# Six blocks of weight quantization in front of a delta-rule scan, and its PSUM banks dealt out anew

## The chip, the core and the metric

The kernel runs on one core of a Trainium2 chip. The metric is the device time of one execution in microseconds (us). The core has five engines with a queue each, worked in order: TensorE for matmuls (PE, with PEld for its weight loads), VectorE (DVE), ScalarE (ACT), GpSimd (POOL) and SyncE (SP), which here only issues transfers. Matmuls write to PSUM, which has eight banks; a bank holds 128 x 512 float32 values.

## The reference

Two transformer-like layers with modulation (`adaLN`) over 2 sequences of 1024 tokens of width 512. Only the first layer's first half bears on this change.

```python
mod = (silu(c0) @ wmod0).reshape(2, 6, 1, 512)      # sa, ca, ga, sb, cb, gb of layer 0
h = layernorm(x) * (1 + ca) + sa
x = x + ga * L0_attn(h)          # delta rule: k, q, v, alpha from h; a 64 x 64 state per sequence
h = layernorm(x) * (1 + cb) + sb
x = x + gb * L0_ffn(h)           # weights made ternary in groups of 64 rows
...
def ternary_quant(w, g=64):      # in bf16
    scale = clip(mean(abs(w_g)), 1e-8)
    q = clip(round(w_g / scale), -1, 1)
    return q * scale
```

The delta rule is a scan over tokens: each step reads the state with q and k, forms an error, a "surprise" gate from it, and updates the state. `L0_ffn` is silu(gate) * up, an RMS norm, and a projection; its `w_gate_up` (4096 x 512) and `w_proj` pass through `ternary_quant`. The second layer (an RWKV-like scan and a feed-forward part with integer weights) follows with modulation vectors of its own.

## The kernel before

**The scan of layer 0.** The 1024 tokens of each sequence are cut into NC = 16 chunks of TT = 64; both sequences lie side by side on the 128 partitions. GT = 2 chunks form a group, so there are NG = 8 groups. A group passes four functions:

- `project(g)` (L309): layer norm on DVE, POOL and ACT, transposes on PE (`pt_a`), the modulated `hTa` on ACT (L338), the projections `pk` (L346) and `pv` (L360), and the normalised `kqr` on DVE (L385, L386).
- `pairs(g, ...)` (L389): the interactions of a chunk's tokens among each other, by doubling over six levels. It starts with `kl` (L396) and `pd`; each level is a PE product `pg`, a predicated copy (L419) and three products on DVE (L428, L431, L437). At its end come `pe`, `pm2`, `pse`, `pki` and `pik`, each followed by one ACT or DVE instruction. All of these PE results have the one tag `pg` in pool `ps_g` with one buffer, so that one bank holds them, one after another.
- `delta_chunk` (L536), twice: about ten short steps between PE, ACT and DVE (`wa` L544, the squares L486, `rt` L494, `r` L496, the new state `h` L518, `w` L553), and checks `miss` and `size` for a fallback branch, which is not run with these inputs.
- `attention_out` (L590): `pssy`, a power on POOL (L236), two products `poa`, and for each a residual on DVE (`res_a`, L229) and an addition to x on POOL (L230). `poa` has one PSUM buffer.

Beside these, two kinds of filling work belong to a group: `modulation(n)` (L680), which makes the next n of ten modulation vectors (sixteen matmuls at L149, a copy at L154, then L161 or L171 and their readers), and `quantize(n)` (L697), which takes the next n of 32 blocks of `w_gate_up` through `ternary` (L649). A block is a load of 256 KB on SP's queue (`qst`, two buffers), Abs and Sign on ACT (`q_ab` L659, `q_sg` L661), one matmul that sums over 64 rows (`pm`, L663), a scaled copy on ACT (`q_sc`, L665), five DVE instructions (`q_d` and `q_m`, L669 to L674) and a cast on ACT (L675). The PSUM results of modulation and quantization share pool `ps_q`, with two buffers.

The order of the main loop, and how far ahead things are written, is this:

```python
ops = [pairs(0, *project(0))]
modulation(1)
ahead = [project(1)]
for g in range(NG):
    ...                       # two delta_chunks of group g
    ...                       # pairs up to g + 2, project up to g + 3, attention_out(g)
    modulation((1, 1, 1, 1, 1, 2, 1, 1)[g])
    quantize(ND)              # ND = 4 blocks
```

**What sets the order on an engine.** The order of the statements is not yet that of the queues. When the kernel is built, a planner deals the instructions to each engine's queue by its own estimate of when they are ready, and among those that are ready the one written earlier goes first. So filling work slips between steps of a chain, and a part of the text written further up gets precedence. On the chip each queue then runs strictly as dealt.

**PSUM in the scan.** Pools: `ps_p` 2 banks (projections), `ps_g` 1 (pairs), `ps_q` 2, `ps_u` 2 (chunks), `ps_o` 1 (outputs). When the scan is over, the pool stack `sp` is closed and the banks go to the feed-forward part, whose first transposes and whose tile `hh` (L219) wait until the scan's tiles are let go.

**Loads of x.** `load_x(c0, c1)` issues one transfer for each sequence. Chunks 0 and 1 are loaded first, then, after the first weights, chunks 2 and 3, and right behind them chunks 4 to 15 at once.

Of the kernel before, what the change touches and what calls it, by code (L numbers as in the profile page):

```python
# [8 lines left out]
F32 = mybir.dt.float32  # L9
# [5 lines left out]
PSUM = bass.MemoryType.PSUM  # L15

P = 128
B, S, D = 2, 1024, 512
ND = D // P
TT = 64  # L20

NC = S // TT
GT = 2
# [19 lines left out]
def block_pair_kernel(ctx: ExitStack, tc: tile.TileContext, a: dict, out: bass.AP):  # L43
    nc = tc.nc

    def pool(stack, name, bufs=1, **kw):
        return stack.enter_context(tc.tile_pool(name=name, bufs=bufs, **kw))
# [66 lines left out]
    def run(general, rs):  # L114
# [136 lines left out]
        with ExitStack() as la:  # L251
# [5 lines left out]
            sp = ExitStack()  # L257
# [1 line left out]

            ps_p = pool(sp, "ps_p", bufs=2, space=PSUM)  # L260
            ps_g = pool(sp, "ps_g", bufs=1, space=PSUM)
            ps_q = pool(sp, "ps_q", bufs=2, space=PSUM)
            ps_u = pool(sp, "ps_u", bufs=2, space=PSUM)
            ps_o = pool(sp, "ps_o", bufs=1, space=PSUM)
            proj = work = pool(sp, "proj", bufs=1)
# [123 lines left out]
            def pairs(g, kqr, al, v):  # L389

                gm = gms[g % 3]
                kqv = kqr.rearrange("p i (j t) -> p i j t", j=GT)
                gmv = gm.rearrange("p (j i) t -> p j i t", j=GT)
                kl = pair.tile([P, GT, TT], F32, tag="kl", name=f"kl_{g}", bufs=2)
                klf = kl.rearrange("p j t -> p (j t)")
                nc.vector.scalar_tensor_tensor(  # L396
                    klf, al, 1.0, kqr[:, 0], ALU.subtract, ALU.mult
                )

                pd = ps_g.tile([P, GT, TT], F32, tag="pg", name=f"pd_{g}")  # L400
                for j in range(GT):
                    both(pd[:, j], kl[:, j], kqv[:, 1, j])
                nc.vector.copy_predicated(
                    gmv[:, :, 2, :], mdiag.unsqueeze(1).to_broadcast([P, GT, TT]), pd
                )

                tot = al
                for h in LEVELS:  # L410
                    nb = TT // (2 * h)
                    ps = ps_g.tile([P, GT, 3, TT // 2], F32, tag="pg", name=f"pg_{g}_{h}")
                    right = kqr.rearrange("p i (n two h) -> p i n two h", two=2, h=h)[:, :, :, 1, :]
                    for j in range(GT):
                        both(
                            ps[:, j].rearrange("p i (n h) -> p i n h", h=h), kl[:, j],
                            right[:, :, j * nb:(j + 1) * nb, :],
                        )
                    nc.vector.copy_predicated(  # L419
                        gm.rearrange("p i (n two h) -> p i n two h", two=2, h=h)[:, :, :, 1, :],  # L420
                        masks[h].rearrange("p (n h) -> p n h", h=h).unsqueeze(1).to_broadcast(
                            [P, GT * 3, nb, h]
                        ),
                        ps.rearrange("p j i (n h) -> p (j i) n h", h=h),
                    )
                    tv = tot.rearrange("p (n two) -> p n two", two=2)
                    left = klf.rearrange("p (n two h) -> p n two h", two=2, h=h)[:, :, 0, :]
                    nc.vector.tensor_tensor(  # L428
                        left, left, tv[:, :, 1].unsqueeze(2).to_broadcast([P, GT * nb, h]), ALU.mult
                    )  # L430
                    nc.vector.tensor_tensor(  # L431
                        right, right,
                        tv[:, :, 0].unsqueeze(1).unsqueeze(3).to_broadcast([P, 3, GT * nb, h]),
                        ALU.mult,
                    )
                    nxt = pair.tile([P, GT * nb], F32, tag=f"tot{h}", name=f"tot_{g}_{h}")
                    nc.vector.tensor_tensor(nxt, tv[:, :, 0], tv[:, :, 1], ALU.mult)  # L437
                    tot = nxt
                atot = scan.tile([P, GT], F32, tag="atot", name=f"atot_{g}", bufs=3)
                nc.vector.tensor_copy(atot, tot)  # L440
                pe = ps_g.tile([P, GT, 3, TT], F32, tag="pg", name=f"pe_{g}")
                for j in range(GT):
                    both(pe[:, j, 0], kl[:, j], eye)
                    both(pe[:, j, 1], gmv[:, j, 0], eye)
                    both(pe[:, j, 2], kqv[:, 0, j], eye)

                kem = scan.tile([P, GT, 3, TT], F32, tag="kem", name=f"kem_{g}", bufs=3)
                nc.scalar.copy(kem, pe)

                im = pair.tile([P, GT, TT], F32, tag="im", name=f"im_{g}")  # L450
                nc.gpsimd.tensor_tensor(
                    im, gmv[:, :, 0], eye.unsqueeze(1).to_broadcast([P, GT, TT]), ALU.add
                )
                pm2 = ps_g.tile([P, GT, TT], F32, tag="pg", name=f"pm2_{g}")
                for j in range(GT):
                    both(pm2[:, j], gmv[:, j, 0], kem[:, j, 1])
                m2 = pair.tile([P, GT, TT], F32, tag="m2", name=f"m2_{g}")
                nc.scalar.copy(m2, pm2)
                pse = ps_g.tile([P, GT, TT], F32, tag="pg", name=f"pse_{g}")
                for j in range(GT):  # L460
                    both(pse[:, j], m2[:, j], im[:, j])
                inv = scan.tile([P, GT, TT], F32, tag="inv", name=f"inv_{g}", bufs=3)
                nc.vector.tensor_tensor(inv, pse, im, ALU.add)

                pki = ps_g.tile([P, GT, 2, TT], F32, tag="pg", name=f"pki_{g}")
                for j in range(GT):
                    both(pki[:, j, 0], kem[:, j, 2], inv[:, j])
                    both(pki[:, j, 1], inv[:, j], eye)
                ki = scan.tile([P, GT, 2, TT], F32, tag="ki", name=f"ki_{g}", bufs=3)
                nc.scalar.copy(ki, pki)  # L470
                pik = ps_g.tile([P, GT, TT], F32, tag="pg", name=f"pik_{g}")
                for j in range(GT):
                    both(pik[:, j], ki[:, j, 1], kem[:, j, 0])
                ik = scan.tile([P, GT, TT], F32, tag="ik", name=f"ik_{g}", bufs=3)
                nc.scalar.mul(ik, pik, 0.5)
                return gmv, kqv, kem, inv, atot, v, ki, ik
# [123 lines left out]
            def scan_all(chunk, p, name):  # L600
                h = p.tile([P, DS], F32, tag="h", name=f"h_init{name}")
                nc.vector.memset(h, 0.0)
                state[0] = h
                ops = [pairs(0, *project(0))]
                modulation(1)
                ahead = [project(1)]
                for g in range(NG):
                    yT = scan.tile([P, GT, TT], F32, tag="yT", name=f"yT_{g}{name}")
                    ysq = scan.tile([P, GT, TT], F32, tag="ysq", name=f"ysq_{g}{name}")
                    for j in range(GT):  # L610
                        chunk(GT * g + j, j, ops[g], yT, ysq)

                    for n in range(len(ops), min(g + 3, NG)):
                        ops.append(pairs(n, *ahead[n - 1]))
                        if n == g + 1:
                            attention_out(g, yT, ysq, f"{g}{name}")
                        for n in range(len(ahead) + 1, min(n + 2, NG)):
                            ahead.append(project(n))
                    if g:
                        attention_out(g, yT, ysq, f"{g}{name}")  # L620
                    modulation((1, 1, 1, 1, 1, 2, 1, 1)[g])
                    quantize(ND)
# [21 lines left out]

            nc.vector.tensor_scalar(wo, wo, nw, -1.0, ALU.mult, ALU.mult)
            load_x(GT, 2 * GT)
            load_x(2 * GT, NC)

            def ternary(dst, src, psp, tag, name):  # L649

# [29 lines left out]
            def modulation(n):  # L680

                for layer, key in later[:n]:
                    if key == "sa1":
                        mods["sc1"] = cond(1)
                    i = ("sa", "ca", "ga", "sb", "cb", "gb").index(key[:2])
                    sc = mods["sc1"] if layer else sc0
                    rows = mod_rows(load_wmod(layer, i, nc.sync), ps_q, "q", sc, key, w0a)
                    if key[0] == "g":
                        to = w0a if key == "ga0" else const if layer else w0
                        mods[key] = mod_gate(rows, ps_q, "q", key, to)  # L690
                    else:
                        mods[key] = mod_cols(rows, ps_q, "q", key, key[0] == "c")
                del later[:n]
# [340 lines left out]
        with ExitStack() as lr:  # L1034
# [105 lines left out]
            ahead = tokens(1)  # L1140
# [208 lines left out]
```

## Time and profile before

| | |
|---|---|
| median of 3 runs | 1224.29 us (1224.22 to 1228.45) |
| the profiled execution | 1233.09 us, of which its span 1231.2 us |
| PE busy | 1138.4 us, 92% of the span |
| PEld busy | 854.5 us, 69% |
| DVE busy | 730.3 us, 59% |
| ACT busy | 636.8 us, 52% |
| POOL busy | 410.4 us, 33% |
| first matmul of `gu` (L762) | at 299.65 us |

All durations below come from the one profiled execution, which took 0.7% longer than the median. Busy shares are means over stages that differ much, so each stage has to be read by itself. A busy PE is one that has matmuls in its pipeline, not one at its peak. The granted clock of PE (PEclk) is given as a share of full speed. In the chain of waits each piece is what released the next one, followed back from the last instruction.

### The profile page before, as it was taken

Reading aid. Unit: us, or ns where it says so; the run is one execution under the profiler, and the core shown is the slowest. Engines: PE = TensorE matmul, PEld = TensorE weight load, DVE = VectorE, ACT = ScalarE, POOL = GpSimd, SP = SyncE. Lnnn points to the kernel's source line nnn. Section 1 sums busy time; section 2 is a strip of 40 time slices with the busy share of each in tenths; the row PEclk is TensorE's granted clock in tenths of the full one; section 3 lists DMA queues with packets and bytes.
Section 4 is the critical chain, followed back from the end, with each engine's and each line's share of the span. In section 5 each row is a group of like instructions: output and inputs, shape, how many; then the busy total and the mean of one; then the engine's idle time right before and its main releaser. Section 6 shows DMA issues by size and latency. Waiting matters only on the chain.

```text
span 1231.2 us, 17856 instructions
## 1 busy us (share of the span) xinstructions
PE 1138.4 (92%) x6746; PEld 854.5 (69%) x6746; DVE 730.3 (59%) x1509; ACT 636.8 (52%) x1423; POOL 410.4 (33%) x350
## 2 busy tenths in 40 slices
PE   5899999987999899999999979989899799999996
PEld 3667667554776688788788755737566488888884
DVE  3377677788777722622422789979899724242322
ACT  3367666567666533433433687876655644242421
POOL 1020112223444644644644313213212424242422
PEclk9899899876999999999999979979999899999998
DMA  8432121311110000000002311110000101010101
GB/s 204 113 87 71 35 89 62 127 54 35 52 43 26 1 1 1 1 1 1 1 35 69 95 35 35 52 35 1 1 1 10 43 26 35 1 35 1 35 1 38
DMA packets 40975, 48.72 MB, mean 40 GB/s; under 512 B 11568, under 2 KB 24880, under 8 KB 40880
## 3 DMA queue, kind: packets, MB, share of 16 engines
q1 hardware_dynamic: 39504, 45.92, 13.0%
q10 hardware_dynamic: 1376, 1.57, 0.4%
q8 instruction: 55, 0.90, 0.3%
q14 instruction: 40, 0.33, 0.1%
HBM read 43.28 MB, written 4.19 MB: 39 GB/s over the span
## 4 chain that ended last, share of the span: by engine, by line
PE 64%; DVE 21%; ACT 9%; issue 3%; POOL 2%; DMA 1%; SPq 1%; DVEq 0%; ACTq 0%
PE gu L762 14%; PE gui L1234 13%; PE pof L749 6%; PE poi L1214 6%; PE pow L1122 3%; PE pk L346 2%; PE pkvr L974 2%; DVE nd L1095 2%; PE u L305 2%; DVE q_m_p L671 2%; DVE xm L965 2%; PE pg L305 2%; PE poa L305 1%; PE pv L360 1%; DVE q_d_p L669 1%
## 5 line engine op out<-in xcount | busy, mean ns | idle before, releaser
L762 PE MATMUL gu<-hh,wgu 128*128 128x512 f32 x512 | 204.6, 402 | 4.9 <-DVE sg L771 3.5
L762 PE MATMUL gu<-hl,wgu 128*128 128x512 f32 x512 | 201.2, 395 | 4.0 <-DVE hl L221 2.7
L1234 PE MATMUL gui<-hp,wi 128*128 128x512 f32 x704 | 165.9, 390 | 0.0
L1234 PEld LDWEIGHTS gui<-hp,wi 128*128 128x128 f32 x704 | 131.8, 188 | 28.2 <-issue 0.8
L777 POOL TENSOR_TENSOR h0l<-sg,h0h 128x512 fp32r<-128x512 f32 x64 | 82.7, 1293 | 168.9 <-ACT h0h L775 168.9
L771 DVE TENSOR_TENSOR sg<-gu,sg 128x512 f32<-128x512 f32 x64 | 44.0, 687 | 139.9 <-ACT sg L770 136.6
L762 PEld LDWEIGHTS gu<-hh,wgu 128*128 128x128 f32 x512 | 97.3, 190 | 30.6 <-DVE sg L771 8.4
L762 PEld LDWEIGHTS gu<-hl,wgu 128*128 128x128 f32 x512 | 96.6, 189 | 27.1 <-DVE hl L221 4.5
L1249 POOL TENSOR_TENSOR h1l<-th,h1h 128x512 fp32r<-128x512 f32 x44 | 56.7, 1289 | 139.9 <-ACT h1h L1247 139.9
L1242 DVE SCALAR_TENSOR_TENSOR th<-th,gui 128x512 f32<-128x512 f32 x44 | 30.2, 687 | 121.7 <-ACT th L1241 121.7
L775 ACT CAST h0h<-sg 128x512 fp32r<-128x512 f32 x64 | 39.7, 621 | 86.8 <-DVE sg L773 84.9
L783 POOL TENSOR_TENSOR acc<-acc,hq 128x512 f32<-128x512 f32 x60 | 83.7, 1396 | 0.0
L1122 PE MATMUL pow<-w_wo,rw 128*64 128x512 f32 x256 | 73.5, 665 | 10.4 <-DVE rw L1113 10.0
L770 ACT ACTIVATE sg<-gu 128x512 f32<-128x512 f32 x64 | 38.1, 595 | 81.4 <-PE gu L762 81.4
L749 PE MATMUL pof<-wp,h0h 128*128 128x512 f32 x256 | 69.3, 392 | 1.7 <-ACT wp L675 1.7
L749 PE MATMUL pof<-wp,h0l 128*128 128x512 f32 x256 | 68.7, 389 | 0.0
L974 PE MATMUL pkvr<-xm,w_wk 128*128 128x256 f32 x256 | 62.1, 397 | 7.0 <-DVE xm L965 7.0
L1241 ACT ACTIVATE th<-gui,hsgate 128x512 f32<-128x512 f32 x44 | 30.3, 689 | 71.7 <-PE gui L1234 71.7
L1247 ACT CAST h1h<-th 128x512 fp32r<-128x512 f32 x44 | 27.3, 622 | 77.2 <-DVE th L1244 77.2
L974 PEld LDWEIGHTS pkvr<-xm,w_wk 128*128 128x128 f32 x256 | 48.3, 195 | 23.8 <-DVE xm L965 12.2
L974 PE MATMUL pkvr<-xm,w_wv 128*128 128x256 f32 x256 | 57.1, 380 | 1.0 <-DVE xm L965 1.0
L974 PE MATMUL pkvr<-xm,w_wr 128*128 128x256 f32 x256 | 56.6, 379 | 0.0
(368 smaller groups left out, 2497.6 us busy)
## 6 DMA issues: line engine op xcount, KB each, us to landing
wm<-in_wmod SPq DMA_DIRECT2D x22, 512.0 KB, 4.6
qst_gu<-in_wgu SPq DMA_DIRECT2D x32, 256.0 KB, 2.7
qst_p<-in_wp SPq DMA_DIRECT2D x16, 256.0 KB, 2.5
out<-oi SPq DMA_DIRECT2D x28, 128.0 KB, 2.4
xs<-in_x SPq DMA_DIRECT2D x2, 1536.0 KB, 15.8
kvt<-in_wq_gate SPq DMA_DIRECT2D x8, 256.0 KB, 2.6
kvt<-in_wq_up SPq DMA_DIRECT2D x8, 256.0 KB, 2.6
ist<-in_wq_down SPq DMA_DIRECT2D x7, 256.0 KB, 2.5
```

The lines of the kernel that those rows point to most:

```text
L305: nc.tensor.matmul(to[rows], weights[rows], moving[rows], start=start, stop=stop, **kw)
L749: nc.tensor.matmul(pos[j], part[:, j * P:(j + 1) * P], wp[i // 4][:, i % 4, :], start=(i == 0 and z == 0), stop=(i == NH0 - 1 and z == 1),)
L762: nc.tensor.matmul(o, wgu[i // 4][:, d, s, (i % 4) * P:(i % 4 + 1) * P], part[:, d], start=(n == 0), stop=(n == 2 * ND - 1),)
L771: nc.vector.tensor_tensor(sg, gu[0], sg, ALU.mult)
L775: nc.scalar.copy(h1, h)
L777: nc.gpsimd.tensor_tensor(h2, h, h1.bitcast(F32), ALU.subtract)
L783: nc.gpsimd.tensor_tensor(acc, acc, hq, ALU.add)
L974: nc.tensor.matmul(ps[:, c * B:(c + 1) * B].rearrange("p b t -> p (b t)"), wkvr[i][:, d, (2 * z + c) * P:(2 * z + c + 1) * P], xm[d].rearr ...
L1122: nc.tensor.matmul(po[b * TT:(b + 1) * TT], rw[:, c, b, j * TT:(j + 1) * TT], wo1[:, c, :], start=(c == 0), stop=(c == ND - 1),)
L1214: nc.tensor.matmul(pos[j], part[:, j * P:(j + 1) * P], wdi[i // HS][:, i % HS, :], start=(i == 0 and z == 0), stop=(i == NH1 - 1 and z == ...
L1234: nc.tensor.matmul(o, wgi[i // HS][:, d, s, (i % HS) * P:(i % HS + 1) * P], part[:, d], start=(d == 0 and z == 0), stop=(d == ND - 1 and z ...
L1249: nc.gpsimd.tensor_tensor(h2, h, h1.bitcast(F32), ALU.subtract)
```

## The change

Four things are altered. The PSUM tiles of `pairs` get the tags `pg0` and `pg1` by the group's parity, so that even and odd groups have a bank each. `ps_q` goes from two banks to one, so the sum stays at eight. In `scan_all`, project(1) is written ahead of modulation(1), with two blocks of quantization between them and four behind. The load of chunks 4 to 15 is cut in two and moved from the place behind chunks 2 and 3 to before and behind those four blocks. The calls `quantize(ND)` in the loop stay; as there are 32 blocks in all, group 6 now finds two left and group 7 none.

```diff
-            ps_q = pool(sp, "ps_q", bufs=2, space=PSUM)
+            ps_q = pool(sp, "ps_q", bufs=1, space=PSUM)
...
-                pd = ps_g.tile([P, GT, TT], F32, tag="pg", name=f"pd_{g}")
+                pd = ps_g.tile([P, GT, TT], F32, tag=f"pg{g % 2}", name=f"pd_{g}")
...
-                    ps = ps_g.tile([P, GT, 3, TT // 2], F32, tag="pg", name=f"pg_{g}_{h}")
+                    ps = ps_g.tile([P, GT, 3, TT // 2], F32, tag=f"pg{g % 2}", name=f"pg_{g}_{h}")
...
                 ops = [pairs(0, *project(0))]
+                ahead = [project(1)]
+                quantize(2)
                 modulation(1)
-                ahead = [project(1)]
+                load_x(2 * GT, 4 * GT)
+                quantize(4)
+                load_x(4 * GT, NC)
                 for g in range(NG):
...
             load_x(GT, 2 * GT)
-            load_x(2 * GT, NC)
```

The tiles `pe`, `pm2`, `pse`, `pki` and `pik` change their tag in the same way as `pd`.

More of the change, by code (lines that the diff above doesn't have):

```diff
@@ L440, in pairs @@
                 nc.vector.tensor_copy(atot, tot)
-                pe = ps_g.tile([P, GT, 3, TT], F32, tag="pg", name=f"pe_{g}")
+                pe = ps_g.tile([P, GT, 3, TT], F32, tag=f"pg{g % 2}", name=f"pe_{g}")
                 for j in range(GT):
@@ L453, in pairs @@
                 )
-                pm2 = ps_g.tile([P, GT, TT], F32, tag="pg", name=f"pm2_{g}")
+                pm2 = ps_g.tile([P, GT, TT], F32, tag=f"pg{g % 2}", name=f"pm2_{g}")
                 for j in range(GT):
@@ L458, in pairs @@
                 nc.scalar.copy(m2, pm2)
-                pse = ps_g.tile([P, GT, TT], F32, tag="pg", name=f"pse_{g}")
+                pse = ps_g.tile([P, GT, TT], F32, tag=f"pg{g % 2}", name=f"pse_{g}")
                 for j in range(GT):
@@ L463, in pairs @@
                 nc.vector.tensor_tensor(inv, pse, im, ALU.add)
-                pki = ps_g.tile([P, GT, 2, TT], F32, tag="pg", name=f"pki_{g}")
+                pki = ps_g.tile([P, GT, 2, TT], F32, tag=f"pg{g % 2}", name=f"pki_{g}")
                 for j in range(GT):
@@ L470, in pairs @@
                 nc.scalar.copy(ki, pki)
-                pik = ps_g.tile([P, GT, TT], F32, tag="pg", name=f"pik_{g}")
+                pik = ps_g.tile([P, GT, TT], F32, tag=f"pg{g % 2}", name=f"pik_{g}")
                 for j in range(GT):
```

## The prediction

> **What bounds the kernel now.** I read the page first (busy rows and slices), then the busy time in five stretches of the scan, then the chain of waits at the scan's end, then the groups of the quantization and the timeline around two of its waits.
>
> ```profile
> span 1231.2 us, 17856 instructions
> PE   5899999987999899999999979989899799999996
> DVE  3377677788777722622422789979899724242322
> PEclk9899899876999999999999979979999899999998
> ```
>
> A slice is 30.8 us. The scan of layer 0 fills the first ten; the first matmul of its feed-forward part starts at 299.65 us. PE is near full nearly everywhere, but slices 9 and 10 have a low granted clock, and DVE is at 7 and 8 there. What follows (feed-forward, the second layer) the diff does not touch, so all of it should move as one piece with the scan's end. I split the scan; the columns are PE, PEld, DVE, ACT, POOL busy, clock, DMA:
>
> ```profile
> 28.00:64.00 36.00, 30.92 (x325) 24.73 (x327) 14.46 (x59) 12.20 (x29) 3.88 (x5) 0.81 0.44 115
> 64.00:208.00 144.00, 141.29 (x1720) 98.22 (x1717) 105.29 (x362) 100.09 (x301) 26.47 (x28) 0.94 0.24 71
> 208.00:240.00 32.00, 29.18 (x347) 18.92 (x346) 24.69 (x88) 17.02 (x61) 7.29 (x6) 0.89 0.29 94
> 240.00:272.00 32.00, 27.98 (x332) 17.99 (x328) 26.64 (x80) 21.03 (x67) 5.14 (x5) 0.84 0.26 84
> 272.00:300.00 28.00, 21.63 (x139) 10.69 (x138) 24.69 (x62) 17.86 (x56) 7.80 (x7) 0.68 0.08 27
> ```
>
> Three regimes. From 28 to 64 us the first projections and pairs form a chain: DVE has 36 - 14.5 = 21.5 us free, ACT 23.8. From 64 to 208 PE is busy 98%: nothing there is gained by moving DVE work. From 240 DVE fills up (88% in the last 28 us) while PE falls to 77% at clock 0.68. The chain of waits says what DVE does there:
>
> ```profile
> 275.30 1.41 DVE q_m_gu L673
> ...
> 278.38 0.33 DVE q_m_gu L673
> ...
> 290.52 0.75 DVE res_a L229
> ...
> 291.61 1.68 DVE q_d_gu L669
> ...
> 294.75 1.41 DVE q_m_gu L673
> ...
> 298.97 0.63 ACT hh L219
> ```
>
> Quantization (q_d, q_m) sits in the last 25 us of the chain, between the residuals of the last chunks. Its cost per block:
>
> ```profile
> L669 DVE SCALAR_TENSOR_TENSOR q_d_gu<-q_sc_gu,q_ab_gu 128x512 bf16<-128x512 bf16 x32 | 25.4, 797 | 2.6 <-ACT q_sc_gu L665 2.6
> L673 DVE TENSOR_TENSOR q_m_gu<-q_m_gu,q_sg_gu 128x512 bf16<-128x512 bf16 x32 | 16.5, 515 | 0.0
> L674 DVE TENSOR_TENSOR q_m_gu<-q_d_gu,q_m_gu 128x512 bf16<-128x512 bf16 x32 | 15.4, 481 | 0.0
> L671 DVE TENSOR_TENSOR q_m_gu<-q_d_gu,q_ab_gu 128x512 bf16<-128x512 bf16 x32 | 15.0, 472 | 0.0
> L672 DVE TENSOR_TENSOR q_d_gu<-q_ab_gu,q_d_gu 128x512 bf16<-128x512 bf16 x32 | 13.5, 423 | 0.0
> ```
>
> DVE pays 797 + 515 + 481 + 472 + 423 = 2.69 us a block. The ACT groups of the same stretch (L659, L661, L665, L675) give 629 + 626 + 597 + 617 = 2.47 us, and PE one pm matmul, 0.39 us.
>
> **Part 1: six blocks leave the end.** There are 32 blocks, four after each of eight groups. With six made in front, groups 0 to 5 still make four each, group 6 two, group 7 none. So 6 x 2.69 = 16.1 us of DVE and 14.8 us of ACT leave the last 40 us. Not all of it is on the path:
> - Chunk 14: its PE result is there at about 270.7; its square runs on ACT at 272.66, behind q_ab, q_sg, q_sc and a cast (2.0 us). Its th is there at 273.2, yet r (L496) starts at 280.04. In that gap DVE runs 2.75 us of q work between the two residuals and 1.7 us after them, but also waits for poa (1.7 us) and does two residuals (1.4 us). Removable: 2.0 + 2.75 + 1.7 = 6.4 us. What is late next is poa of chunks 12 and 13 on PE, which the modulation's L149 matmuls precede, so I count 5.5.
> - After h of chunk 15: 0.4 us before w, 0.4 before the last residual, 0.1 where the transposes wait for the last q_sc, and 2.0 where hh (298.97) waits for DVE's queue to reach "good" (L712), behind seven q instructions. Sum 2.9, counted 3.
> So -8.5. Bounds: 0 (poa and the chunks' own chain hold everything) and -16.1 (all of DVE's share).
>
> Whether PE also speeds up there is open. Its clock reads 0.50 from 288 to 304; four poa matmuls take 1.97 us there against about 1.07 at full clock, and the sixteen transposes 3.67. If the clock came back, two poa and the transposes would give another -2 x 0.9 - 1.8 = -3.6. The Trainium skill ("TensorE: Matmul & The Clock Gate", What's actually happening) says the array falls to half rate after about 3.4 us of idling and rises only after as long a busy stretch. The PE waits of this tail come from the residual's hops (PE, DVE, PE), which stay; by the rule 0. I take 0, and keep -3.6 for the range.
>
> **Part 2: a second bank for the pairs.** Only one group's pairs can be under way now.
>
> ```profile
> 218.41 0.28 DVE L386 TENSOR_TENSOR kqr<-kqr,al 128x128 f32<-128x128 f32 x1
> ...
> 228.07 0.28 DVE L396 SCALAR_TENSOR_TENSOR kl<-al,kqr 128x128 f32<-128x128 f32 x1
> ```
>
> In DVE's timeline the inputs of the last pairs are ready at 218.7, but it starts at 228.07, just after pik of the pairs before. That is 9.4 us, and in front 4.4 (kl at 56.2, its first pd at 60.67). Little of it is end time: from 64 to 208 PE is full anyway. In front PE has 1.3 us idle between 56 and 60; late, the wa of chunk 12 waits on DVE from about 245.6 to 256.23 partly behind this pairs' work. From the trace, 0 to -6. The same page of the skill (HAM oscillation) reports a kernel that got no further gain from PSUM double-buffering; by that rule 0, and the total would be 2 us later. I take -2: PE is not full after 208, which is where a second bank counts.
>
> **Part 3: six blocks in front.** 16.1 us go into 21.5 free on DVE, 14.8 into 23.8 free on ACT, 6 x 0.39 = 2.3 into PE's 5.1 idle. Both engines run their queue in order, so a chain step can find a q instruction running: some 20 DVE steps x 16.1/36 x half of 0.54 us = 2.4, some 10 ACT steps x 14.8/36 x 0.31 = 1.3, PE 2.3; at most 6. But the chain matters only where PE then lacks work, and project(1), now written ahead of modulation(1), and the earlier pairs give it some. Bounds 0 and +6; I take +1.5. If that idle time were not there, the blocks would cost their full 16.1.
>
> The queues: SP issues six loads of 256 KB earlier, and x from chunk 4 in four transfers, not two. Now the rest of x (3 MB) goes first:
>
> ```profile
> 19.22 13.70 SPq L136 DMA_DIRECT2D wm<-in_wmod  x4
> 32.97 5.94 SPq L657 DMA_DIRECT2D qst_gu<-in_wgu  x2
> ```
>
> SP needs 13.7 us for four issues behind a full queue, and the first two blocks leave at 33. Ahead of that x they can leave near 18; the slowest qst load took 11.1 us to land, so 29 at worst. If ACT reached one at 24, hTa would stand behind it: up to 5 us, in the range, not the sum. The later x pieces are safe: chunks 4 and 5 are first read at 58.55 (st_a). Two more issues are 2 x 0.66 us of SP, which has none due. POOL gets nothing new; its pow steps wait for DVE and are in the DVE count.
>
> **Part 4: one bank for quantization and modulation.** A modulation holds a bank from its first L149 to its last reader: 72.5 to 88.6, 141.9 to 164.4, 201.3 to 221.2, about 13 us in the mean, ten times. Blocks used the other bank; now they queue behind it, and each pm waits for the q_sc before it. Ten modulations x 13 plus 32 blocks x 2.5 (pm 0.39, q_sc 0.60, and an estimated 1.5 until ACT comes) = 210 of 260 us: it fits. The price is on PE, which runs in order: a pm that waits holds up pairs and chunks. The trace has no such wait. The nearest row is the reverse one:
>
> ```profile
> ACT q_sc_gu L665 <- PE pm_gu L663: 12.4, 14, 2.1
> ```
>
> 14 waits of 0.89 us. Lower bound 0 (pm issued only when the bank is free), upper 24 blocks x 0.89 = 21. I take +1.5, nearer the lower end, because DVE's 2.69 us a block, not the bank, paces a block.
>
> **Sum.** -8.5 - 2 + 1.5 + 1.5 = -7.5 us on the profiled execution's 1233.09, that is 1225.6. The median shown, 1224.29, is 0.7% below that execution; scaled, 1216.8.
>
> **Rivals.**
> *No gain (0.20).* The last chunks' own chain sets the end: of part 1 only the 2.9 us after h of chunk 15 come off, part 2 gives 0, parts 3 and 4 cost 3. Then 1224. For it: between h of chunks 14 and 15 there are 4.2 us with little q work in the path. Against: chunk 14 takes 14.9 us, three times that.
> *Slower (0.25).* PE waits at pm for the one bank. With the 0.89 us of the row above at each of the 24 blocks between 64 and 272 us: +21; with -8.5 for the tail, -2 for the pairs and +1.5 in front: +12, so 1236. It decides from 9 / 24 = 0.38 us a block, where it eats the gain. For it: PE is busy 98% from 64 to 208, so no stall can hide. Against: a block comes every 8 us there, and its predecessor's q_sc is long done unless a modulation intervenes.
> *It does nothing of the kind* (inside the 0.20): the six blocks, though written first, run after the first chunks, as those written after group 0 start on ACT only at 70.45 though loaded by about 44. The end would still have six fewer.
>
> **How the numbers follow.** A measurement of this kernel can tell about 0.5%, 6.1 us, from no change. Main case 0.55: 1206 to 1218, likeliest 1216.8. Faster by over 0.5% is below 1218.2: most of the main case and a little of the first rival, 0.55. Within 0.5%: 0.20. Slower: 0.25. The range goes down to 1204 (-16 tail, -3.6 clock, -2 pairs, +1.5 in front is 1204) and up to 1238, which takes in the slower rival's price.
>
> **What would show it.** The first gu matmul near 292, not 299.65; q instructions between 35 and 70 us; no q_d in the last 20 us of the scan; r of chunk 14 within 4 us of its th; kl of the last pairs within 3 us of its kqr; waits of PE at L663 under 4 us in all. Wrong if PE's share from 64 to 208 falls under 96%, if pm waits top the list, or if the pairs of group 0 end over 5 us later than 60.3.

## The result, and the profile after

| | before | after |
|---|---|---|
| median | 1225.48 us (1224.22 to 1228.45, 5 runs) | 1233.20 us (1230.91 to 1235.84, 5 runs) |
| profiled execution, its span | 1233.09, 1231.2 us | 1231.09, 1228.2 us |
| first matmul of `gu` | 299.65 us | 298.18 us |

The change makes the kernel slower: ratio 1.0054, 95% interval 1.0031 to 1.0077, about 6.6 us. The two profiled executions stand the other way round only because that of before was 0.6% above its median; a second profile of the same kernel (run x1 below) has its first `gu` at 295.85. In both, in the changed kernel and in runs x2 to x4, 929.5 to 933.4 us of the span come after that matmul, and the changed kernel's 930.0 us are 1.5 less than the 931.5 of both profiles of before. So the loss is made in the scan. From `ternary` on, lines have moved down by three.

The page of the changed kernel, its span and the rows of PE, DVE and clock in 40 slices of 30.7 us:

```profile
span 1228.2 us, 17843 instructions
PE   5899999996999899999999979989899799999996
DVE  3685687777777722622422789979899724242322
PEclk8888899987999999999999979979999899999999
```

DVE's second slice went from 3 to 6: the six blocks are made in front. Slices 9 and 10, low on clock before (7 and 6), are a little better (8 and 7), but slices 1, 3 and 4 are lower, and PE's slice 10 fell from 7 to 6. The stretches of the scan (columns as before: PE, PEld, DVE, ACT, POOL, clock, DMA share, GB/s):

```profile
28.00:64.00 36.00, 29.58 (x310) 20.46 (x306) 23.07 (x80) 23.25 (x52) 3.86 (x4) 0.87 0.53 130
64.00:208.00 144.00, 135.03 (x1610) 94.55 (x1610) 105.20 (x353) 95.70 (x283) 27.08 (x28) 0.93 0.24 68
208.00:240.00 32.00, 29.72 (x384) 20.82 (x386) 25.88 (x85) 19.91 (x68) 5.78 (x6) 0.95 0.25 76
240.00:272.00 32.00, 29.49 (x333) 18.84 (x333) 24.70 (x82) 17.21 (x60) 5.30 (x5) 0.95 0.32 100
272.00:300.00 28.00, 19.96 (x176) 9.71 (x177) 19.17 (x49) 13.08 (x51) 8.25 (x7) 0.77 0.01 1
```

The front took the blocks in (DVE 14.46 to 23.07) and the tail lost some (24.69 to 19.17), as foreseen. The loss is in the second row: PE is busy 135.03 of 144 us, 93.8%, where it was 141.29; that is 6.3 us of new idle time in a stretch that had none to give. Not all of it comes from the banks: with the front alone (x4 below) PE is busy 138.08 us there, so 3.2 us came with the front. The chain of waits at the end still has a block in it:

```profile
277.05 0.75 DVE res_a L229
277.80 0.33 DVE q_m_gu L677
278.14 1.68 DVE q_d_gu L672
...
280.94 0.33 DVE q_d_gu L675
281.27 1.41 DVE q_m_gu L676
282.68 0.20 DVE r L496
```

Though six fewer blocks were left for the end, the steps of the last two stand in front of `r` of chunk 14 (282.68). The block itself costs what it did, and PE hardly waits for the one bank at `pm` (groups of 28 to 300 us; after the bar busy us and mean ns, then idle time before it and its releasers):

```profile
L672 DVE SCALAR_TENSOR_TENSOR q_d_gu<-q_sc_gu,q_ab_gu 128x512 bf16<-128x512 bf16 x32 | 25.1, 789 | 2.3 <-ACT q_sc_gu L668 2.0
L666 PE MATMUL pm_gu<-q_ab_gu,bones_h 128*128 128x512 bf16 x32 | 13.5, 421 | 4.4 <-ACT q_ab_gu L662 3.9 <-DVE ga L176 0.3 <-ACT q_sc_gu L668 0.2
```

### The profile page after: what moved, and what is told of

Same layout as the page of the kernel before. It is cut to its first block, busy times and chain, and to the rows that moved or that the text cites. A ratio compares the mean times of both kernels' runs of the same rounds, so it can differ in the third digit from the quotient of the medians.

```text
span 1228.2 us, 17843 instructions
## 1 busy us (share of the span) xinstructions
PE 1129.7 (92%) x6746; PEld 849.7 (69%) x6746; DVE 732.4 (60%) x1509; ACT 637.9 (52%) x1423; POOL 410.2 (33%) x350
## 4 chain that ended last, share of the span: by engine, by line
PE 61%; DVE 22%; ACT 9%; issue 3%; POOL 2%; DMA 1%; SPq 0%; DVEq 0%; ACTq 0%; POOLq 0%
PE gu L765 14%; PE gui L1237 13%; PE pof L752 7%; PE poi L1217 6%; PE pow L1125 3%; DVE nd L1098 2%; PE pkvr L977 2%; PE pk L346 2%; DVE xm L968 2%; PE u L305 2%; DVE q_m_p L674 2%; PE pg L305 2%; PE poa L305 1%; PE pv L360 1%; DVE q_d_p L672 1%
```

## The account: idle PE and lowered clock

From 28 us to the first `gu` every kernel does the same work. The window up to each kernel's own first `gu`, of the kernel before (x1), then of the changed one:

```profile
28.00:295.85 267.85, 246.76 (x2843) 169.04 (x2839) 194.81 (x644) 166.89 (x509) 50.27 (x50) 0.89 0.26 77
```

```profile
28.00:298.18 270.18, 242.27 (x2806) 163.57 (x2803) 196.20 (x643) 168.36 (x509) 48.83 (x49) 0.91 0.27 74
```

DVE (195, 196) and ACT (167, 168) do not vary. What varies is PE's idle time (the window less its busy time), 267.85 - 246.76 = 21.1 and 270.18 - 242.27 = 27.9 us, and what the lowered clock costs, by estimate (1 - 0.89) x 267.85 = 29.5 and (1 - 0.91) x 270.18 = 24.3. Taking both off leaves 217 and 218 us. The account is a rough one. The clock is rounded to 0.01, so each loss is good to 1.5 us; a low clock while PE has no work is counted too; and over the rows below 213 to 221 us are left, so up to 8 us of a difference can stay unexplained.

Each of these windows is from one execution. A second measure uses all: every timed execution has its span and its mean granted clock, and (1 - clock) x span is an estimate of the clock loss of the whole kernel. The last two columns give its median and that of the span without it. The kernel before stands at 60.0 and 1164.4 in the executions timed beside x1, and x1, the same kernel, at 56.4 and 1168.4, so differences under 4 us say nothing here.

| kernel (banks of ps_q; pairs) | ratio, 95% interval | first gu | PE idle to gu | clock loss to gu | clock loss, all executions | the rest |
|---|---|---|---|---|---|---|
| x1: before again | 1.0000 (0.9978 to 1.0023) | 295.85 | 21.1 | 29.5 | 56.4 | 1168.4 |
| x4: front alone (two, as before; one) | 0.9948 (0.9925 to 0.9970) | 291.31 | 25.6 | 18.4 | 47.5 | 1171.9 |
| x3: one bank alone (one, shared; one) | 1.0065 (1.0043 to 1.0087) | 305.33 | 27.9 | 30.5 | 63.6 | 1170.6 |
| x2: banks alone (one, shared; two) | 1.0127 (1.0100 to 1.0155) | 306.59 | 26.3 | 39.0 | 70.8 | 1168.4 |
| x5: front, one bank (one, shared; one) | 1.0097 (1.0072 to 1.0123) | 310.13 | 28.3 | 39.5 | 67.5 | 1171.9 |
| after (one, shared; two) | 1.0054 (1.0031 to 1.0077) | 298.18 | 27.9 | 24.3 | 54.1 | 1174.9 |
| x7: front, banks apart (one and one; one) | 0.9895 (0.9868 to 0.9921) | 289.45 | 19.2 | 20.9 | 43.7 | 1168.7 |

Both measures say the same of the changed kernel: it lost nothing to the clock. Its clock loss is below that of before, and what it loses is idle PE, 27.9 us up to the first `gu` against 21.1. The low clock sets x2 and x5 apart, and the high one x4 and x7.

## The experiments

Ratios are against the kernel before on the same chip, as in the table.

**x1, the kernel before again**, for a second profile.

> The kernel of before itself, as a measure of the spread and for a second profile of it. The profile of before took 1233.1 us, its timed runs 1224.2 to 1228.5; that of after 1231.1, its runs 1230.9 to 1235.8, so the two profiles do not show the 0.54% between the medians. Ratio 1.000 within 0.3%. If the profiled execution of before was an unlucky one, this profile ends near 1225 and its first gu matmul starts near 292 instead of 299.65; if the timed difference lies outside the scan, it starts near 299 again.

**x2, the banks alone**, and **x3, the single bank alone**:

```diff
-            ps_q = pool(sp, "ps_q", bufs=2, space=PSUM)
+            ps_q = pool(sp, "ps_q", bufs=1, space=PSUM)
```

x2 has the tags `pg0` and `pg1` as well, x3 not.

> Only the PSUM banks of the change: pairs of even and odd groups a bank each, quantization and modulation one bank; no block in front, loads of x as before. Theory A (the single bank makes PE and the blocks wait, and the second pairs bank gives nothing): slower than before by 8 to 16 us. Theory B (the blocks in front cost in the front what they save at the end): within 2 us of before. The prediction's own terms: -2 for the pairs, +1.5 for the bank, so -0.5.

> Only ps_q from two banks to one; the pairs keep their one bank, so one bank lies idle. Theory A: slower by 8 to 16 us, as much as with the pairs' second bank. Theory B: within 2 us of before. The prediction's term: +1.5, at most +21.

**x4, the front alone**: the changed kernel's `scan_all` and loads, the banks of before.

> Only the six blocks in front, project(1) ahead of modulation(1) and the divided load of x; PSUM banks as before. Theory A: 6 to 9 us faster than before, the gain that the single bank then eats. Theory B: slower than before by 5 to 9 us, as the whole change is. The prediction's terms: -8.5 + 1.5, so -7.

Measured: 1241.80, 1236.36 and 1220.97 us where before has 1226.56. The front gains 0.5%, as the prediction had it for parts 1 and 3; the single bank loses 0.65%, and the second pairs bank loses 0.6% more on top. The theory that the front costs what it saves falls. In x3 PE also stands for the bank, 4.0 us in all by the blocks' `q_sc` as releaser, most of it where a modulation begins:

```profile
278.50 1.11 PE L149 MATMUL ps_gb<-wm,scp 128*64 128x256 f32 x2 [2.19 <-ACT q_sc_gu L665]
```

**x5 to x8, what about the bank.** x5 is the changed kernel with the pairs back on `pg`. x6 is the kernel before, and x7 x5's front, with a bank each for blocks and modulation (`ps_q` with one buffer for each of two tags):

```diff
-                    rows = mod_rows(load_wmod(layer, i, nc.sync), ps_q, "q", sc, key, w0a)
+                    rows = mod_rows(load_wmod(layer, i, nc.sync), ps_q, "m", sc, key, w0a)
```

(and the same tag in `mod_gate` and `mod_cols`). x8 is the changed kernel with `ps_p, "pp"` in those three places.

> The changed kernel with the pairs back on one bank: six blocks in front, one bank for blocks and modulation, one for the pairs (seven banks used). Theory 1 (blocks queue behind the modulation that holds the shared bank; the second pairs bank costs nothing or little): as the changed kernel, 1230 to 1236 us where the kernel before has 1226. Theory 2 (the second pairs bank takes precedence from the chunks and costs 5 us more, as the difference of the two runs without the front suggests): 1224 to 1230. With front alone at 1221, the distance from it is the price of one bank, the distance to the changed kernel the price of the pairs' bank.

> The kernel before with the two banks of ps_q dealt out, one for the blocks and one for modulation. If the price of the single bank is that a block must wait for a modulation to be read out (theory 1): as before, 1224 to 1229, and no pm after a long hold at the end of the scan. If it is that a block must wait for the block before it (theory 3): as with one bank, 1233 to 1237.

> Six blocks in front as in the changed kernel, one bank for the pairs, one for the blocks and one for modulation. Theory 1: as front alone, 1219 to 1223 (ratio 0.995), or a little better since two blocks never hold both banks when a modulation comes. Theory 3: 1226 to 1232. If the front itself depends on blocks overlapping each other, it loses 2 to 4 us.

> The changed kernel, but the ten modulations inside the scan take their PSUM from the two banks of the projections, as the first two modulations do; the blocks keep the one bank of ps_q to themselves, and the pairs keep two. Theory 1: the loss goes, 1220 to 1226; what remains over front alone is the second pairs bank. Theory 2: 5 us over front alone remain, near 1226. If a modulation now holds up the projections instead: 1232 to 1240.

Measured: x5 1240.94; x6 1221.96, ratio 0.9959 (0.9930 to 0.9987); x7 1216.03; x8 1228.14, ratio 1.0003 (0.9987 to 1.0020). With the same single bank for the blocks, x6 is 1.1% faster than x3, and x7 2% faster than x5: that a block waits for the block before it costs nothing (x6 is even faster than before), that it shares the bank with modulation costs. x7 beats both kernels. The order of the two on PE at the scan's end, in the changed kernel (start, length, then line and tile), shows what sharing looks like:

```profile
257.79 0.61 PE L666 MATMUL pm_gu<-q_ab_gu,bones_h 128*128 128x512 bf16 x1
...
264.96 0.38 PE L666 MATMUL pm_gu<-q_ab_gu,bones_h 128*128 128x512 bf16 x1
266.57 0.65 PE L149 MATMUL ps_cb<-wm,scp 128*64 128x256 f32 x2
...
271.56 0.38 PE L666 MATMUL pm_gu<-q_ab_gu,bones_h 128*128 128x512 bf16 x1
273.14 0.51 PE L666 MATMUL pm_gu<-q_ab_gu,bones_h 128*128 128x512 bf16 x1
276.89 0.65 PE L149 MATMUL ps_gb<-wm,scp 128*64 128x256 f32 x2
```

and in x7:

```profile
251.77 0.39 PE L666 MATMUL pm_gu<-q_ab_gu,bones_h 128*128 128x512 bf16 x1
252.09 0.65 PE L149 MATMUL ps_cb<-wm,scp 128*64 128x256 f32 x4
...
258.18 0.38 PE L666 MATMUL pm_gu<-q_ab_gu,bones_h 128*128 128x512 bf16 x1
259.52 0.65 PE L149 MATMUL ps_gb<-wm,scp 128*64 128x256 f32 x2
261.48 0.61 PE L666 MATMUL pm_gu<-q_ab_gu,bones_h 128*128 128x512 bf16 x1
262.02 1.12 PE L149 MATMUL ps_gb<-wm,scp 128*64 128x256 f32 x4
```

With a bank each the blocks fall between the matmuls of one modulation. With one for both they are dealt as runs: some blocks, a whole modulation, some blocks. The last `pm` comes at 273.14 and not at 261.48, and the last modulation begins 17.4 us later. It is the same further up: the sixteen matmuls of `ps_gb` start between 122.1 and 153.8 us in x7, and between 145.9 and 151.4 in the changed kernel.

How a run of blocks can hurt is best seen at 91 us of the changed kernel, where two blocks are in DVE's queue at once between the short steps `tot` of the pairs (DVE's timeline):

```profile
91.97 0.16 DVE L437 TENSOR_TENSOR tot<-tot 128x8 f32<-128x8 f32 x1
92.22 0.69 DVE L672 SCALAR_TENSOR_TENSOR q_d_gu<-q_sc_gu,q_ab_gu 128x512 bf16<-128x512 bf16 x1
92.83 0.15 DVE L437 TENSOR_TENSOR tot<-tot 128x4 f32<-128x4 f32 x1
92.90 0.42 DVE L674 TENSOR_TENSOR q_m_gu<-q_d_gu,q_ab_gu 128x512 bf16<-128x512 bf16 x1
93.24 0.15 DVE L437 TENSOR_TENSOR tot<-tot 128x2 f32<-128x2 f32 x1
93.31 0.42 DVE L674 TENSOR_TENSOR q_m_gu<-q_d_gu,q_ab_gu 128x512 bf16<-128x512 bf16 x1
```

PE's timeline shows it out of work meanwhile (x5 has the same gap of 1.85 us; x4, with the same front and two shared banks, one of 0.57), and the four windows around it show the clock:

```profile
93.41 1.22 PE L377 MATMUL pr<-ident,rb 128*128 128x128 f32 x4 [1.85 <-DVE tot L437]
```

```profile
88.00:92.00 4.00, 3.53 (x54) 2.55 (x53) 3.95 (x18) 3.68 (x8) 1.25 (x2) 1.00 0.02 4
92.00:96.00 4.00, 2.13 (x8) 1.51 (x8) 2.56 (x11) 1.14 (x4) 0.92 (x1) 0.54 0.22 66
96.00:100.00 4.00, 3.55 (x28) 2.32 (x28) 2.44 (x9) 3.49 (x10) 0.00 (x0) 0.50 0.00 0
100.00:104.00 4.00, 3.97 (x48) 3.21 (x44) 2.00 (x11) 3.05 (x5) 0.00 (x0) 0.68 0.20 60
```

A low clock went along with this gap: 4 x (0.46 + 0.50 + 0.32) = 5.1 us are lost to it, about 10 us at half. The Trainium skill ("TensorE: Matmul & The Clock Gate", What's actually happening) states the drop for about 3.4 us of idling; here the longest gap was 1.85 us, with two of 0.46 and 0.45 behind it. But its length did not decide it. If the clock fell once, from 1.00 to 0.50, the mean of 0.54 from 92 to 96 puts the fall at about 92.3, when the gap had lasted 0.8 us. x8 and x9 have one and the same gap there, and only x8 a low clock (PE's timeline, then the window, of each):

```profile
92.73 0.79 PE L377 MATMUL pr<-ident,rb 128*128 128x128 f32 x2 [1.29 <-ACT rb L374]
92.00:104.00 12.00, 11.27 (x95) 8.23 (x97) 6.95 (x30) 8.89 (x21) 1.64 (x3) 0.57 0.07 23
```

```profile
92.95 0.49 PE L377 MATMUL pr<-ident,rb 128*128 128x128 f32 x2 [1.29 <-ACT rb L374]
92.00:104.00 12.00, 10.93 (x142) 8.34 (x142) 9.70 (x40) 10.86 (x25) 1.86 (x3) 1.00 0.14 45
```

And two executions of the kernel before, its profile and x1, have PE busy throughout at the same time of the scan, one at half the clock:

```profile
128.60:138.70 10.10, 10.10 (x59) 5.08 (x59) 5.16 (x14) 3.79 (x8) 3.24 (x4) 0.50 0.17 54
```

```profile
128.60:138.70 10.10, 10.10 (x106) 5.58 (x108) 7.74 (x20) 6.32 (x17) 4.83 (x5) 1.00 0.18 54
```

So the clock of one stretch in one execution is not yet a property of the kernel. That x5's clock is lower than x7's does not rest on one profile: in six timed executions of each it was 0.944 to 0.950 and 0.956 to 0.964 over the whole span.

x5 loses most in a stretch without a long gap. From 104 to 128 us:

```profile
104.00:128.00 24.00, 23.68 (x340) 17.98 (x339) 12.85 (x54) 15.97 (x56) 2.64 (x3) 1.00 0.22 69
```

From 128 to 156 us, x5 and then x7:

```profile
128.00:156.00 28.00, 26.59 (x187) 16.73 (x188) 16.85 (x46) 11.52 (x29) 4.92 (x5) 0.55 0.06 19
```

```profile
128.00:156.00 28.00, 27.75 (x367) 20.21 (x369) 21.24 (x73) 18.70 (x55) 6.78 (x7) 1.00 0.13 39
```

From 128 us on x5's PE is nearly as busy as x7's, does half the matmuls, and 0.45 x 28 = 12.6 us are lost to the clock: half of the difference between the two kernels. In the 24 us before it PE was idle for 0.3 us, so no idle time explains this fall. What does is not shown.

**x9 to x12, the pieces of the front and the pairs' bank.** x9 is x8 with the pairs on one bank. The other three are x7 with one edit each: `quantize(8)` for `quantize(4)` (x10, ten in front); all of x loaded ahead as in the kernel before (x11); and (x12)

```diff
+                modulation(1)
                 ahead = [project(1)]
                 quantize(2)
-                modulation(1)
```

> Modulation in the projections' two banks and six blocks in front, as in the run before (1228, ratio 1.0003), but the pairs back on one bank, so that the second pairs bank is the only thing taken away. If the second bank costs something by itself: faster than 1228, about 1221 to 1224, near front alone. If it gives something here, as it did beside the shared bank (1241 without, 1233 with): 1231 to 1236. If it is worth nothing either way, and what is left over front alone is the price of modulation among the projections: 1226 to 1230.

> Six in front and blocks and modulation apart gave ratio 0.9895, with no q_d after 265 us. Here ten in front. If the gain comes from blocks leaving the scan's end: nothing more to be had, 0.988 to 0.992, or a loss of up to 5 us where the four more blocks meet the pairs in front. If each block in front is worth 1 us wherever it came from: 4 us faster, 0.986.

> The best kernel so far (six in front, banks apart, ratio 0.9895) with all of x loaded first, as in the kernel before, so that the first weight block leaves at about 33 us and not at 17. If the early loads matter: the six blocks come later, among the first chunks, and 3 to 6 us are lost (0.992 to 0.995). If only the place in the text matters: 0.988 to 0.991.

> The best kernel so far with modulation(1) written ahead of project(1), as in the kernel before; the blocks stay in front. If the order of the two matters little: 0.988 to 0.991. If project(1) was what gave PE work beside the first pairs: group 1's pairs start 3 us or more later and 2 to 4 us are lost (0.991 to 0.993).

Measured: x9 1220.11, ratio 0.9952 (0.9924 to 0.9980); x10 1234.93, 1.0061 (1.0029 to 1.0093); x11 1231.16, 1.0032 (1.0017 to 1.0048); x12 1224.42, 0.9980 (0.9961 to 0.9999). The second pairs bank costs again (x8 against x9). The other three lost far more than any theory said: 0.85% to 1.7% against x7, 10 to 20 us. The clock alone makes 13 to 14 us (57.8, 56.5 and 57.8 us lost in the median of all executions of x10, x11 and x12, where x7 loses 43.7). For x11 the row of the front shows a part of it:

```profile
28.00:64.00 36.00, 31.14 (x312) 24.38 (x310) 14.15 (x55) 14.77 (x35) 3.71 (x4) 0.69 0.38 91
```

DVE has 14.15 us there, where x7 has 22.64, and the clock is 0.69, where x7 has 0.93: with x loaded first the first `q_d` starts at 62.0 us, so the blocks went in among the first chunks after all, though written in front. In x10 they are where they should be (ten `q_d` between 35.3 and 74.1), and the pairs of group 2 begin at 105.7 instead of 99.0.

**x13 to x18, the bank or the luck of the order.** If any edit of the order moves the time by 1%, two runs prove little of a bank. So the three other fronts were run with the shared bank too (x13 to x15), two of them with the second pairs bank as well (x16, x18), and the kernel before with nothing but `ahead = [project(1)]` put ahead of `modulation(1)` (x17).

> Ten blocks in front, blocks and modulation on one shared bank, pairs on one bank. With the banks apart this front took ratio 1.0061 (1235). If sharing is itself the cause of the loss: 10 us or more on top, 1.014 to 1.025. If the loss was the luck of the order: anywhere from 0.995 to 1.015, on either side of 1.006.

> Six blocks in front with all of x loaded first, one shared bank, pairs on one bank. With the banks apart: ratio 1.0032 (1231). Sharing the cause: 1.011 to 1.023. Luck of the order: either side of 1.003.

> Six blocks in front with modulation(1) ahead of project(1), one shared bank, pairs on one bank. With the banks apart: ratio 0.998 (1224). Sharing the cause: 1.006 to 1.018. Luck of the order: either side of 0.998.

> The changed kernel with all of x loaded first, thus with the shared bank and the second pairs bank. The second pairs bank gained 5 us beside the shared bank with the early loads, and cost 6 us without a front and beside a bank of the blocks' own. If it relieves a kernel whose blocks are late: 4 to 8 us under the run of this call with x first and one pairs bank. If its sign is the luck of the order: either way.

> The kernel before with the two lines modulation(1) and ahead = [project(1)] swapped, nothing else. Behind the six blocks in front the same swap gave 1224.4 to 1216.0, 0.85%. If project(1) first gives PE work in front: 0.992 to 0.998. If such an edit only deals the order anew: anywhere from 0.993 to 1.010, with a loss as likely as a gain.

> The changed kernel with modulation(1) ahead of project(1), thus with the shared bank and the second pairs bank. With one pairs bank: ratio 0.9999 (1226). If the second pairs bank costs, as in three pairs of four: 1.004 to 1.007. If its sign is the luck of the order: 0.995 to 1.007.

Measured: x13 1.0068 (1.0046 to 1.0089), x14 1.0073 (1.0044 to 1.0101), x15 0.9999 (0.9982 to 1.0017), x16 1.0124 (1.0094 to 1.0155), x17 0.9986 (0.9962 to 1.0010), x18 1.0052 (1.0035 to 1.0068). Side by side, as ratios:

| front | blocks and modulation apart | shared | shared, two pairs banks |
|---|---|---|---|
| none | 0.9959 (x6) | 1.0065 (x3) | 1.0127 (x2) |
| six, as in the change | 0.9895 (x7) | 1.0097 (x5) | 1.0054 (after) |
| six, modulation first | 0.9980 (x12) | 0.9999 (x15) | 1.0052 (x18) |
| six, x first | 1.0032 (x11) | 1.0073 (x14) | 1.0124 (x16) |
| ten | 1.0061 (x10) | 1.0068 (x13) | |

Sharing never gains: +1.1%, +2.0%, +0.2%, +0.4% and +0.1%, of which the first two lie clear outside the intervals. The other three were expected to lose 0.8% or more if sharing were itself the cause, and none did. Sharing costs most where the order with the banks apart is good, and next to nothing where that order is poor already. In the timed executions its part outside the clock is never a gain (4.6, 3.2, 11.5, 2.7 and 0.4 us, in the rows' order), while its part in the clock goes either way (+9, +24, -9, +2 and +3), each good to about 4 us. So it is mostly the clock that makes an order costly (x7 to x5) or cheap (x12 to x15). The second pairs bank costs 0.5 to 0.6% in three of the four rows, and in the fifth comparison (x9 to x8, 0.5%); in the changed kernel alone it gains, 0.4%, against the costliest of the orders with one pairs bank (x5). Swapping the two lines alone (x17) is worth nothing.

## Why the prediction was wrong

It said 1216.8 and faster; it was 1233.2 and slower, inside the range. By its parts, on 1226 us:

- **Parts 1 and 3, -7: right in size, in part by luck.** The front alone gave -0.52%, -6.4 us (x4), with the banks apart -0.64% (x6 to x7) and beside two pairs banks -0.72% (x2 to the changed kernel), but beside the shared bank and one pairs bank it cost 0.3% (x3 to x5). In x4 the first `gu` came at 291.31, as foreseen. But it came so by the clock, the term that the prediction put at 0: in the median of all executions x4 loses 47.5 us to it and before 60.0, while the rest is 7.5 us longer (x4's PE is idle 25.6 us up to the first `gu`, x1's 21.1). In the changed kernel the q instructions stood in front as foreseen (`q_d` at 40.8 to 65.1 us), and the pairs of group 0 ended 3.2 us earlier, not later. Two things were not weighed enough: that the early loads decide whether the blocks come in front (x11, without them, is 1.4% or 17 us slower than x7; the prediction saw only a transfer that lands sooner), and that the gain is tied to one order (x10, x12).
- **Part 4, +1.5: the step that failed.** "Nearer the lower end, because DVE's 2.69 us a block, not the bank, paces a block." The bank did not pace a block, that much is right (x6), nor did PE stand at `pm` for it: 0.2 us in all. But the term was mis-sized. It measured +8 us alone (x3; 5 to 11 by the interval) and, from x4 to x5, 1.0097 / 0.9948, 1.5%, or 18 us. Its upper bound of 21 held it; I chose the wrong end. The step looked only at waits of `pm`. PE's waits for the bank at the modulations' own first matmuls are 1.3 us in the changed kernel and 3.1 in x3, where with `pm`'s 0.9 they are 4.0 of the 6.8 us that PE is idle longer than in x1. The rest of the price came with another order: blocks in runs between whole modulations. That such a run meets short steps on DVE and idles PE is seen at 91 us; that runs make the whole of the rest is argued, not shown. Nor is it shown why the clock, 21 of the 24 us between x4 and x5 in the account, is so much lower in x5.
- **Part 2, -2: wrong in sign outside of this kernel, too small in it.** From x5 to the changed kernel -0.43%, -5 us; in four other comparisons +6 to +8 (-5 is within reach of no change: the intervals of x5 and of the changed kernel overlap). That gain is one of clock, 67.5 to 54.1 us in the median of all executions, with the rest 3 us longer. The sign named for success, `kl` of the last pairs within 3 us of its `kqr`, failed: with a bank free, DVE still comes to it 10.1 us later.

```profile
223.81 0.28 DVE L386 TENSOR_TENSOR kqr<-kqr,al 128x128 f32<-128x128 f32 x1
233.92 0.28 DVE L396 SCALAR_TENSOR_TENSOR kl<-al,kqr 128x128 f32<-128x128 f32 x1
```

So it was not the bank that kept the last pairs waiting. In x9, with one pairs bank, the same step comes 1.3 us after its input (222.21 and 223.55). What was weighed against it, a kernel that gained nothing by a second PSUM buffer (the Trainium skill, "TensorE: Matmul & The Clock Gate", HAM oscillation), was nearer than my reading of the timeline, and still too kind.

In sum -6.4 + 18 - 5 = +6.6. That this meets the measured 1.0054 proves nothing: steps of one path from before over x4 and x5 to the changed kernel must add up to it. Over x3 and x2 the parts are +8, +8 and -9. The slower rival named 1236, close by, but by a mechanism that the profile denies (PE standing 0.89 us at each `pm`). The threshold set for being wrong, PE under 96% from 64 to 208 us, was met with 93.8%, but it does not single out the shared bank: x8, where blocks and modulation share no bank, has 134.93 us there, and x4, which gains, 138.08, just under 96%. Of the lesser signs, the first `gu` came at 298.2, not 292; the last `q_d` came at 280.94 (L675), 17.2 us before it and within the 20 us that should have been free; `r` came 3.9 us after its `th` (278.69 to 282.60), within the 4 us; PE's waits at L666 were 4.4 us, not under 4.

What stays open: what lowers the clock in one order and not in another, and why the second pairs bank costs 0.5%. In their profiles x8 idles PE 26.0 us and x9 21.0 us up to the first `gu`, at a clock of 0.91 and 0.92, so that most of it looks like idle time; over all executions x8 loses 52.1 us to the clock and x9 48.2, and the rest differs by 1.4. Which chain of instructions makes it was not isolated. And the share of luck in one order can't be taken out of a single comparison of two kernels here, only out of a row of them.

## What to carry to other kernels

When filling work shares a PSUM bank with an accumulation that holds it for long, the price need not show as a wait on that bank (1.5 us on PE in the changed kernel): look at where the planner puts the work and at what then idles the bound engine, and try a bank each. Here that was never worse, and clearly better in two of five orders. Where PE is the bound, count idle time and clock apart, and the clock over several executions, not from one profile. And where an order is dealt by a planner, test a reason in several orders: single edits that were expected to cost at most 0.5% moved this kernel by 0.85% to 1.7%.

## What the runs showed of the hardware that was not expected

The clock went to half about gaps much shorter than 3.4 us (0.54 from 92 to 96 us of the changed kernel, with a gap of 1.85 us), and also without a gap: 0.50 over 10.1 us in which PE is recorded busy for all 10.1 (the kernel before, from 128.6 us), and 0.55 over 28 us with PE busy for 26.59 (x5). In another execution of that same kernel, x1, the clock was 1.00 at that time, and PE did 106 matmuls and not 59. With the same gap of 1.29 us it fell in x8 and stayed full in x9. So neither the busy share nor the length of a gap told the clock here: the busy share alone would have ranked x5 beside x7 there. A difference in clock between two kernels needs several executions of each.
